# FFN weight tiles turned by a transposing DMA on 16-bit planes, in place of TensorE transposes

## The chip, the cores and the metric

The kernel runs on one core of a Trainium2 chip. The metric is the device time of one execution in microseconds. Five engines work beside each other: TensorE (PE in the profile; its weight loads are PEld), VectorE (DVE), ScalarE (ACT), GpSimd (POOL) and SyncE (SP), which here only issues DMAs. Each engine runs its own instruction list in order and waits on semaphores for the others.

## The reference

One transformer layer on x of 2048 tokens x 1024 features, in float32. First attention across the 32 heads of each token, then a gated FFN whose weights go through a 4-bit quantization and back:

```python
x = x + attn(layernorm(x), wq, bq, wk, bk, wv, bv)
dq(w): per block of 64 values: absmax, idx = searchsorted(bounds, w / absmax), NF4_CODE[idx] * absmax
g, u = y @ dq(w1).T, y @ dq(w2).T          # y = layernorm(x); w1, w2: 2752 x 1024
x = x + (silu(g) * u) @ dq(w3).T           # w3: 1024 x 2752
```

Quantizing and restoring the weights (w1, w2 and w3) is part of the work, and TensorE needs the restored weights transposed.

## The kernel before, in words

**Attention sweep.** The 16 token tiles of 128 rows are swept one after another: layer norm, transposes of the normed rows, q, k and v projections, scores, softmax, weighted sum, residual (`S`, `G`, `keep` and their callers; lines 610 to 865). L770 is the transpose of one tile's attention output on DVE, one for each token tile.

**FFN.** The hidden dimension of 2752 is cut into 21 chunks of 128 and one of 64, in six groups of up to four chunks. For each group and each half of the tokens, `Unit` (line 1406) multiplies chunk by chunk; a unit is seven products of four matmuls each (a Strassen-like scheme, `mm4` at L391), and its last operation on DVE is the multiply at L1451. `down7` (line 1509) multiplies the group's result with the third weight and sends the parts through ACT copies (L1532) and accumulating DMAs of POOL (L1534) into `x1d`. Unit operands come by SP's DMAs: `load_w12` (L458, L459) into two buffers, `load_op` (L446) for x.

**The weights, in the background.** A generator, `background()` (line 283), prepares 65 weight tiles, in an order of jobs ("1", c), ("2", c), ("3", c) and one joint ("12", 21). For each tile:

- `load_w` (L188 to L201) loads 128 x 1024 values into `wn` (three buffers), two jobs ahead.
- `absmax` (L264) takes each block's maximum (L271) and scales the tile by its reciprocal (L259 on ACT, L255 on DVE).
- Eight bands follow: ACT rounds to int8 (L299), DVE adds and clips (L303 for the first, L305 for the others) into `r` (two buffers).
- `scaled` multiplies `r` by the maxima, and `finish` (line 205) is put on a list of pending work.

`finish` transposes `r` on PE in eight 128x128 pieces (L219), four to a PSUM bank, and ACT copies each half into `wop` (L220; one buffer of eight 128x512 slots). After the second weight of a pair, DVE forms four sums (L226 to L229, L232 to L235), and SP stores the slots into a DRAM tile `wd` (L238). Units load from `wd` later.

**The order.** PE's list is the program's order, written by hand. On the other engines a scheduler decides the order when the program is built. The sweep and the units call `advance(n)`, which lets the background take steps at a fixed rate for the PE work just issued, and `flush`, which takes one step of `finish`; each step that issues transposes therefore has its fixed place in PE's list. `until(kind, c)` takes steps until a weight is there.

`hook["scale"]` names the engine that scales `r`: ACT in the attention sweep, then ACT and DVE in turn ("both"), and DVE inside `down7`.

The lines that the change touches:

```python
for half in range(2):
    pt = hook["psum"](half)
    for k in range(4):
        j = 4 * half + k
        nc.tensor.transpose(pt[:q, k, :], v[:, j * q : (j + 1) * q], ident)
    nc.scalar.copy(o[:q, first + half], pt[:q])
    yield
```

Of the kernel before, what the change touches and what calls it, by code (L numbers as in the profile page):

```python
# [20 lines left out]
P = 128  # L21
# [30 lines left out]
NNEG = 7  # L52
I8 = mybir.dt.int8
I32 = mybir.dt.int32
F32R = mybir.dt.float32r
LOW = 0xFFF

# [34 lines left out]
def preln_block_kernel(  # L92
# [22 lines left out]
    c = {"ident": ident, "eps": eps, "mhalf": mhalf}  # L115
    c["flag"] = const.tile([1, 1], I32, name="flag")
    io = (x, wqT, wkT, wvT, qb, kb, vb, w1, w2, w3, out)
# [13 lines left out]
def forward(ctx, tc, const, fast, x, wqT, wkT, wvT, qb, kb, vb, w1, w2, w3, out):  # L131

    nc = tc.nc
    xf = x.flatten_outer_dims()
    of = out.flatten_outer_dims()
    ident, eps, mhalf = const["ident"], const["eps"], const["mhalf"]
# [15 lines left out]
    hook = {"scale": "ACT"}  # L152
# [7 lines left out]
    def behind(kind):  # L160

        last = urgent["last"]
        return tc.issue_after(last) if last and kind in urgent["rule"] else nullcontext()
# [24 lines left out]
    def load_w(kind, c):  # L188
        h0, hn = c * P, min(P, F - c * P)
        t = dqp.tile([P, E], FP, tag="wn", name="wn", bufs=3)  # L190
        if kind == "3":
            nc.sync.dma_start(
                t[:, : KC * hn].rearrange("p (k h) -> p k h", h=hn),
                w3[:, h0 : h0 + hn].rearrange("(k p) h -> p k h", p=P),
            )
        elif kind == "12":
            nc.sync.dma_start(t[:hn, :], w1[h0 : h0 + hn, :])
            nc.sync.dma_start(t[hn : 2 * hn, :], w2[h0 : h0 + hn, :])
        else:
            nc.sync.dma_start(t, (w1 if kind == "1" else w2)[h0 : h0 + hn, :])  # L200
        return t  # L201

    wops = {}

    def finish(kind, c, v):

        hn = min(P, F - c * P)
        q = hn if kind == "3" else P
        paired = kind == "3" and c < PAIRED
        second = kind == "2" or paired and c % 2  # L210
        if not second:
            wops["t"] = dqp.tile([P, 8, 4, P], FP, tag="wop", name="wop", bufs=1)
        o = wops["t"]
        first = 2 if second else 0
        for half in range(2):
            pt = hook["psum"](half)
            for k in range(4):
                j = 4 * half + k
                nc.tensor.transpose(pt[:q, k, :], v[:, j * q : (j + 1) * q], ident)  # L219
            nc.scalar.copy(o[:q, first + half], pt[:q])  # L220
            yield
        if kind == "1" or paired and not second:
            return
        if paired:
            b11, b12, b21, b22, t1, t2, t3, t4 = (o[:, n] for n in range(8))
            nc.vector.tensor_tensor(t1, b12, b11, ALU.subtract)  # L226
            nc.vector.tensor_tensor(t2, b22, t1, ALU.subtract)
            nc.vector.tensor_tensor(t3, b22, b12, ALU.subtract)
            nc.vector.tensor_tensor(t4, b21, t2, ALU.subtract)  # L229
        if kind == "2":  # L230
            a11, a12, a21, a22, s1, s2, s3, s4 = (o[:, n] for n in range(8))
            nc.vector.tensor_tensor(s1, a21, a22, ALU.add)  # L232
            nc.vector.tensor_tensor(s2, s1, a11, ALU.subtract)
            nc.vector.tensor_tensor(s3, a11, a21, ALU.subtract)
            nc.vector.tensor_tensor(s4, a12, s2, ALU.subtract)  # L235
        n = 8 if second else 2
        d = tc.dram_tile([q, n, 4, P], FP, name=f"wd{kind}_{c}")
        nc.sync.dma_start(d, o[:q, :n])  # L238
        wd[kind, c] = d
        if paired:  # L240
            wd[kind, c - 1] = d

    pending, step = [], {}
# [6 lines left out]
    def scaled(dst, src, by, nb, engine):  # L250

        if engine == "DVE":
            d, s = (a.rearrange("p (b e) -> p b e", e=BLOCK) for a in (dst, src))
            f = by[:, :nb].unsqueeze(2).to_broadcast([P, nb, BLOCK])
            nc.vector.tensor_tensor(d, s, f, ALU.mult)  # L255
            return
        with behind("scale"):
            for n in range(nb):
                nc.scalar.mul(dst[:, ts(n, BLOCK)], src[:, ts(n, BLOCK)], by[:, n : n + 1])  # L259

    def width(kind, c):
        return KC * min(P, F - c * P) if kind == "3" else E

    def absmax(kind, c, wn):  # L264

        w = width(kind, c)
        nb = w // BLOCK
        v = wn[:, :w]
        am = fs.tile([P, 16], FP, tag="am", name="am")
        rc = fs.tile([P, 16], FP, tag="rc", name="rc")[:, :nb]  # L270
        nc.vector.tensor_reduce(  # L271
            am[:, :nb],
            v.rearrange("p (b e) -> p b e", e=BLOCK),
            AX.X,
            ALU.max,
            apply_absolute_value=True,
        )
        nc.vector.scalar_tensor_tensor(rc, am[:, :nb], 0.0, am[:, :nb], ALU.is_equal, ALU.add)
        nc.vector.reciprocal(rc, rc)  # L279
        scaled(v, v, rc, nb, "DVE" if hook["scale"] == "DVE" else "ACT")  # L280
        return am

    def background():
        ready = load_w(*jobs[0])
        ahead = load_w(*jobs[1])
        am = absmax(*jobs[0], ready)
        yield
        for n, (kind, c) in enumerate(jobs):
            wn, wa = ready, am
            ready = ahead  # L290
            if n + 2 < len(jobs):
                ahead = load_w(*jobs[n + 2])
            w = width(kind, c)
            v = wn[:, :w]
            r = dqp.tile([P, E], FP, tag="r", name="r", bufs=2)[:, :w]
            for i, (lo, hi, scale, bias) in enumerate(BANDS):
                t = dqp.tile([P, E], I8, tag="sg", name="sg", bufs=6)[:, :w]
                with behind("step"):
                    nc.scalar.activation(t, v, AF.Copy, bias=bias, scale=scale)  # L299
                top = float(NF4_CODE[hi + 1])  # L300
                low = -1.0 if lo is None else float(NF4_CODE[lo])
                if i == 0:
                    nc.vector.tensor_scalar(r, t, top, low, ALU.min, ALU.max)  # L303
                else:
                    nc.vector._custom_dve(TENSOR_ADD_SAT, out=r, in0=r, in1=t, s0=top, s1=low)  # L305
                step["n"] = i
                yield
                if i == 4 and n + 1 < len(jobs):
                    am = absmax(*jobs[n + 1], ready)
                    yield  # L310
            engine = ("ACT", "DVE")[n % 2] if hook["scale"] == "both" else hook["scale"]
            scaled(r, r, wa, w // BLOCK, engine)
            pending.append(finish(kind, c, r))
            yield

    def low_bits():

        acc = dqp.tile([P, E], FP, tag="r", name="acc", bufs=2).bitcast(I32)
        chunks = [(m, k) for m in (wqT, wkT, wvT) for k in range(KC)]
        got = []  # L320

        def load():
            if chunks:
                m, k = chunks.pop(0)
                t = dqp.tile([P, E], FP, tag="wn", name="wn", bufs=3)
                nc.sync.dma_start(t, m[ts(k, P), :])
                got.append(t.bitcast(I32))

# [19 lines left out]
    def chain():  # L348
        yield from background()
        if fast:  # L350
            yield from low_bits()
# [179 lines left out]
    if fast:  # L531
# [22 lines left out]
        def load_W(m):  # L554

            W[m] = [
                (wpool if tag in XTAGS else wv).tile([P, 2, E], F32R, tag=tag, name=f"w{m}{n}")
                for n, tag in enumerate(TAGS[m])
# [51 lines left out]
        def split(i):  # L610

            hi = work.tile([P, KC, P], F32R, tag="xh", name="xh", bufs=2)
            lo = work.tile([P, KC, P], F32R, tag="xl", name="xl", bufs=2)
            src = xn.pop(i)
# [293 lines left out]
    else:  # L908
# [190 lines left out]
        with tc.issue_after(opening["first"]):  # L1099
            for n in range(2):  # L1100
                k = slice(2 * n, 2 * n + 2)
# [4 lines left out]
        for n in range(2):  # L1106
            k = slice(2 * n, 2 * n + 2)
# [27 lines left out]
        def load_A(src, p):  # L1135
            t = pair.tile([P, 7, 4, P], FP, tag="A", name="A", bufs=2)
            nc.sync.dma_start(t, src[p])
            return t

        for p in range(NP):  # L1140
# [33 lines left out]
            if p == NP - 2:  # L1174
                first = load_A(opD, 0)
# [463 lines left out]
    for n, (g, tbp) in enumerate(passes):  # L1639
        half, sides = None, []  # L1640
        while now is not None and now.tbp == tbp and now.c in g:
# [6 lines left out]
            if g[-1] == NFULL and unit.c == NFULL - 1:  # L1648
                half = Half(tbp)
# [61 lines left out]
```

## Time and profile before

| | |
|---|---|
| median of 3 runs | 2228.09 us (2227.78 to 2230.97) |
| the profiled execution | 2224.73 us |
| its span, first to last instruction | 2222.9 us |
| granted TensorE clock, mean | 0.983 |
| PE busy | 2144.0 us (96%) |
| weight loads | 1148.3 us (52%) |
| DVE busy | 1395.8 us (63%) |
| ACT busy | 1302.8 us (59%) |
| POOL busy | 275.4 us (12%) |
| DMA, mean rate | 181 GB/s, 402.73 MB |

The busy time of an engine is the time in which at least one of its instructions ran. A group of the profile is a source line, an engine, an operation and the shapes; it has the count, the busy time, the mean duration of one in nanoseconds, and the idle time of that engine just before these instructions with what ended it ("<-PE ptw L219": the transposes of line 219). A view by stretches gives the busy time of each engine between two moments, for all instructions or for one line. The view of waits gives for each waiting line and each releasing line the total, the number of times and the longest.

### The profile page before, as it was taken

The page shows a single profiled execution, that of the slowest core. Times are in us where ns is not written, and L with a number is a line of the kernel's source. Part 1 is how long each engine was busy: PE and PEld are TensorE (multiplying, and loading weights), DVE is VectorE, ACT ScalarE, POOL GpSimd, SP SyncE. Part 2 cuts the span into 40 slices and gives each one's busy share as a digit, 9 for nine tenths or more (in the row PEclk, how much of TensorE's full clock was granted, in tenths as well). Part 3 has the DMA queues.
Part 4 walks back from the last instruction along what each step waited for, and adds up shares of the span by engine and source line. Part 5 has one row for each costly group of instructions (what it writes and reads, how often), then busy time and mean ns, then how long its engine had stood idle before and what let it go on. Part 6 is the DMA issues. An engine that isn't in the chain of part 4 may idle for free.

```text
span 2222.9 us, 35192 instructions
## 1 busy us (share of the span) xinstructions
PE 2144.0 (96%) x14193; PEld 1148.3 (52%) x14193; DVE 1395.8 (63%) x1599; ACT 1302.8 (59%) x2635; POOL 275.4 (12%) x335
## 2 busy tenths in 40 slices
PE   7899989898999999999999999999999999999998
PEld 6677777776544444444444444444444444444432
DVE  6788877978666567565665756756656656453022
ACT  7667665756656657657657676586575676411200
POOL 1000000000003104013021030030120310401300
PEclk8899999999999999999999999999999999999999
DMA  8132323324669539579377694494983866965972
GB/s 294 40 126 68 116 68 107 119 85 160 239 240 263 140 123 250 191 266 196 125 196 190 247 243 133 148 224 165 320 181 123 182 173 256 259 208 141 259 286 96
DMA packets 154684, 402.73 MB, mean 181 GB/s; under 512 B 13648, under 2 KB 67920, under 8 KB 137360
## 3 DMA queue, kind: packets, MB, share of 16 engines
q1 hardware_dynamic: 113808, 326.92, 40.9%
q0 software_dynamic: 40704, 73.47, 19.6%
q8 instruction: 113, 1.85, 0.3%
q14 instruction: 59, 0.48, 0.1%
HBM read 227.07 MB, written 173.28 MB: 180 GB/s over the span
## 4 chain that ended last, share of the span: by engine, by line
PE 44%; issue 21%; DMA 5%; POOL 2%; DVE 1%; ACT 1%; POOLq 0%; SPq 0%; DVEq 0%; ACTq 0%
PE z L391 17%; PE q L391 8%; PE z L1519 7%; DMA x1d<-acc 4%; PE rr L391 4%; PE y L1519 4%; POOL x1d L1534 2%; PE r L1519 2%; PE po L1602 1%; PE ptw L219 1%; PE po L1613 1%; DMA wn<-in_wqT_dram 0%; DVE r L305 0%; ACT acc L1532 0%; DMA w<-wd 0%
## 5 line engine op out<-in xcount | busy, mean ns | idle before, releaser
L299 ACT ACTIVATE sg<-wn 128x1024 int8<-128x1024 f32 (+1 forms) x520 | 541.8, 1050 | 100.0 <-DVE r L305 87.8
L305 DVE CUSTOM_DVE_ANT_0 r<-r,sg 128x1024 f32<-128x1024 f32 (+1 forms) x455 | 552.0, 1213 | 22.2 <-ACT sg L299 1.6
L1534 POOL DMA_DIRECT2D x1d<-acc x280 | 243.9, 900 | 1247.0 <-ACT acc L1532 1196.8
L391 PE MATMUL z<-xB,w 128*128 128x512 f32 x720 | 323.4, 599 | 8.8 <-DMA w<-wd 4.9
L391 PE MATMUL z<-xT,w 128*128 128x512 f32 x656 | 294.9, 592 | 0.0
L391 PE MATMUL q<-xT,w 128*128 128x512 f32 x656 | 291.3, 592 | 0.0
L1519 PE MATMUL z<-w,h 128*128 128x512 f32 x496 | 231.2, 594 | 3.2 <-ACT acc L1532 3.0
L259 ACT ACTIVATE wn<-wn,rc 128x64 f32<-128x64 f32 x752 | 192.6, 336 | 62.6 <-DVE rc L279 59.1
L391 PEld LDWEIGHTS z<-xB,w 128*128 128x128 f32 x720 | 135.9, 192 | 170.8 <-issue 157.7
L391 PEld LDWEIGHTS q<-xT,w 128*128 128x128 f32 x656 | 123.3, 190 | 149.5 <-issue 147.6
L391 PEld LDWEIGHTS z<-xT,w 128*128 128x128 f32 x656 | 123.0, 190 | 146.8 <-issue 146.1
L1434 DVE TENSOR_TENSOR g<-g,rr 128x512 f32<-128x512 f32 x41 | 27.9, 681 | 210.3 <-PE rr L391 210.2
L220 ACT COPY wop<-ptw 128x512 f32<-128x512 f32 (+1 forms) x130 | 76.1, 586 | 134.8 <-PE ptw L219 122.8
L1519 PEld LDWEIGHTS z<-w,h 128*128 128x128 f32 x496 | 92.4, 190 | 115.4 <-issue 101.2
L303 DVE TENSOR_SCALAR r<-sg 128x1024 f32<-128x1024 int8 (+1 forms) x65 | 44.8, 689 | 169.2 <-PE ptw L219 152.8
L1519 PE MATMUL y<-w,h 128*128 128x512 f32 x320 | 148.8, 592 | 0.0
L391 PE MATMUL rr<-xB,w 128*128 128x512 f32 x328 | 147.5, 592 | 0.0
L1532 ACT COPY acc<-z 128x512 f32<-128x512 f32 x160 | 92.9, 581 | 84.8 <-PE z L1519 48.2
L259 ACT ACTIVATE r<-r,am 128x64 f32<-128x64 f32 x440 | 112.8, 341 | 5.2 <-DVE r L305 4.8
L648 PE MATMUL pj<-wk,xh 128*128 128x512 f32 x224 | 94.1, 420 | 14.8 <-DVE qd L667 14.6
L271 DVE TENSOR_REDUCE am<-wn 128x16 f32<-128x1024 f32 (+1 forms) x65 | 78.3, 1204 | 39.8 <-ACT r L259 37.1
L391 PEld LDWEIGHTS rr<-xB,w 128*128 128x128 f32 x328 | 61.5, 190 | 73.7 <-issue 73.7
(144 smaller groups left out, 2749.2 us busy)
## 6 DMA issues: line engine op xcount, KB each, us to landing
x1d<-acc POOLq DMA_DIRECT2D x280, 256.0 KB, 7.0
wd<-wop SPq DMA_DIRECT2D x31, 2048.0 KB, 9.0
w<-wd SPq DMA_DIRECT2D x41, 1280.0 KB, 7.0
wn<-in_w_dram SPq DMA_DIRECT2D x63, 512.0 KB, 6.1
xT<-xdT SPq DMA_DIRECT2D x28, 1024.0 KB, 7.1
xB<-xdB SPq DMA_DIRECT2D x24, 1024.0 KB, 7.3
w<-wd SPq DMA_DIRECT2D x44, 512.0 KB, 4.1
w<-wd SPq DMA_DIRECT2D x10, 1536.0 KB, 7.3
```

The costliest lines, as they stand in the source:

```text
L220: nc.scalar.copy(o[:q, first + half], pt[:q])
L259: nc.scalar.mul(dst[:, ts(n, BLOCK)], src[:, ts(n, BLOCK)], by[:, n : n + 1])
L271: nc.vector.tensor_reduce(am[:, :nb], v.rearrange("p (b e) -> p b e", e=BLOCK), AX.X, ALU.max, apply_absolute_value=True,)
L299: nc.scalar.activation(t, v, AF.Copy, bias=bias, scale=scale)
L303: nc.vector.tensor_scalar(r, t, top, low, ALU.min, ALU.max)
L305: nc.vector._custom_dve(TENSOR_ADD_SAT, out=r, in0=r, in1=t, s0=top, s1=low)
L391: nc.tensor.matmul(dst, w[:, k, :], xop[:, k, :], start=start and k == 0, stop=stop and k == 3, skip_group_check=True,)
L648: nc.tensor.matmul(ps, part[:, k, :], W[m][k // 2][:, k % 2, ts(n, TB)], start=k == 0 and part is xs[i][0], stop=k == KC - 1 and part is x ...
L1434: nc.vector.tensor_tensor(self.g0, self.g0, r, ALU.add)
L1519: nc.tensor.matmul(dst, side[n][:, ts(q, P)], w3T[g[2 * m]][:, W3[n]], start=start and m == 0, stop=stop and m == 1, skip_group_check=True,)
L1532: nc.scalar.copy(t, src)
L1534: nc.gpsimd.dma_start(x1d[8 * tbp + 2 * q + j][n], t, accum_op=ALU.add)
```

## The change

For the 63 full tiles (not the joint tile of the two 64-row ends, nor the last 64 columns of the third weight), `finish` no longer uses PE. ACT reads `r` as 16-bit halves and writes the low halves of all values, then the high halves, into the tile's old `wn` buffer: two planes of 1024 halves. SP issues one transposing DMA from there into two slots of `wop` that are free at that time. A copy on POOL (while `hook["scale"]` is ACT) or on DVE (otherwise) puts the halves together again into the slots where PE's result used to go. The number of steps of `finish` is the same. `wn` now stays in use until the transposing DMA has read it.

```diff
-    def finish(kind, c, v):
+    def finish(kind, c, v, wn):
...
-        for half in range(2):
-            pt = hook["psum"](half)
-            for k in range(4):
-                j = 4 * half + k
-                nc.tensor.transpose(pt[:q, k, :], v[:, j * q : (j + 1) * q], ident)
-            nc.scalar.copy(o[:q, first + half], pt[:q])
+        if hn == P:
+            planes = wn.bitcast(U16).rearrange("p (two e) -> p two e", two=2)
+            turned = o[:, first + 4 : first + 6].rearrange("p n k d -> p (n k d)").bitcast(U16)
+            nc.scalar.copy(planes, v.bitcast(U16).rearrange("p (e two) -> p two e", two=2))
+            nc.sync.dma_start_transpose(
+                turned.rearrange("p (j h) -> p j h", h=P), wn.bitcast(U16)
+            )
             yield
+            joins = nc.gpsimd if hook["scale"] == "ACT" else nc.vector
+            joins.tensor_copy(
+                o[:, first : first + 2].rearrange("p n k d -> p (n k d)").bitcast(U16)
+                .rearrange("p (e two) -> p two e", two=2),
+                turned.rearrange("p (two e) -> p two e", two=2),
+            )
+            yield
+        else:
+            for half in range(2):
+                pt = hook["psum"](half)
+                for k in range(4):
+                    j = 4 * half + k
+                    nc.tensor.transpose(pt[:q, k, :], v[:, j * q : (j + 1) * q], ident)
+                nc.scalar.copy(o[:q, first + half], pt[:q])
+                yield
...
-            pending.append(finish(kind, c, r))
+            pending.append(finish(kind, c, r, wn))
```

More of the change, by code (lines that the diff above doesn't have):

```diff
@@ L54 @@
 I32 = mybir.dt.int32
+U16 = mybir.dt.uint16
 F32R = mybir.dt.float32r
```

## The prediction

> **What bounds the kernel now.** I read the busy time of each engine over four stretches first, then the same stretches for the TensorE transposes of line 219, then the groups of instructions, then who waited for whom. I cut the span at the sixth attention-output transpose (L770, 254.1 us), the first closing multiply of an FFN unit (L1451, 636.2) and the 23rd (1436.6): W1 and W2 are attention, W3 and W4 the FFN.
>
> ```profile
> 0.00:254.10 254.10, 225.47 (x3889) 180.80 (x3890) 202.41 (x224) 172.99 (x375) 18.03 (x36) 0.92 0.39 132
> 254.10:636.20 382.10, 354.29 (x6348) 263.14 (x6347) 303.17 (x329) 232.62 (x510) 13.45 (x19) 0.98 0.41 138
> 636.20:1436.60 800.40, 797.20 (x2039) 363.95 (x2038) 505.63 (x592) 524.95 (x1025) 121.88 (x140) 1.00 0.67 193
> 1436.60:2222.90 786.30, 767.01 (x1920) 340.37 (x1918) 384.57 (x460) 372.26 (x726) 122.04 (x140) 0.99 0.71 206
> ```
>
> After the length come PE, weight loads, DVE, ACT, POOL (busy us), granted clock, DMA share, GB/s. PE is busy 797 of 800 us in W3 and 767 of 786 in W4: there a microsecond taken off PE is a microsecond of the kernel. In W2 it is 354 of 382, with DVE at 303 (79%) beside it. DVE and ACT have 37% and 34% to spare in W3, 21% and 39% in W2.
>
> ```profile
> 0.00:254.10 254.10, 5.37 (x32) 4.13 (x32) 0.92 0.39 132
> 254.10:636.20 382.10, 10.19 (x68) 8.48 (x68) 0.98 0.41 138
> 636.20:1436.60 800.40, 37.32 (x248) 30.83 (x248) 1.00 0.67 193
> 1436.60:2222.90 786.30, 25.80 (x172) 21.37 (x172) 0.99 0.71 206
> ```
>
> These are line 219 alone: 520 transposes, 78.7 us of PE, 0.151 each.
>
> ```profile
> L219 PE MATMUL ptw<-ident,r 128*128 128x128 f32 x512 | 77.5, 274 | 3.8 <-DVE vd L680 2.0 <-ACT wop L220 1.8
> L220 ACT COPY wop<-ptw 128x512 f32<-128x512 f32 x128 | 75.0, 586 | 128.1 <-PE ptw L219 116.1 <-DMA wd<-wop 12.0
> L303 DVE TENSOR_SCALAR r<-sg 128x1024 f32<-128x1024 int8 x64 | 44.2, 691 | 160.1 <-PE ptw L219 152.8 <-ACT wn L259 7.3
> L299 ACT ACTIVATE sg<-wn 128x1024 int8<-128x1024 f32 x512 | 536.9, 1056 | 98.2 <-DVE r L305 85.9 <-DVE r L303 4.9 <-ACT acc L1532 1.0
> L568 DVE CAST wq<-stage 128x1024 fp32r<-128x1024 f32 x4 | 2.8, 690 | 5.1 <-DMA stage<-in_wqT_dram 5.1
> ```
>
> The reader should stop at L303: DVE sat idle 152.8 us because the first band of the next weight tile waits until PE has transposed an older one out of the two buffers of `r`. PE's order is fixed by hand, so **the transposes are also the pace-maker of the dequantization**, and they go.
>
> **The change, part by part.** The instruction lists of the two programs say what it issues. PE loses 504 of 520 transposes (63 full tiles; the 64-row ones stay): 504 x 0.151 = 76.3 us. PE alone would then need 254.1 - 5.4 = 249, 382.1 - 10.2 = 372, 800.4 - 37.3 = 763 and 786.3 - 23.4 = 763 (the 16 that stay, 2.4 us, are in W4): 2147 in all.
>
> ACT loses 126 copies (0.586 us each, 74 us) and gains 63 splits of 2048 halves. L299 gives 1.056 us for 1024 elements and 0.633 for 512, so a straight line gives 1.9; bounds 1.06 (if halves went at double rate) and 2.1; I take 1.9, as no ACT row shows a faster rate. ACT +46 us.
>
> The joins read 2048 halves and write every second one: 52 on DVE, 11 on POOL. DVE's nearest row is L568 (one SBUF input): 0.690 for 1024, where two-input adds take 0.69 for 512 and 1.22 for 1024, so twice their rate. Bounds: 0.69 (rate doubled again) and 2.29 (single rate); I take 1.22, L568's rate. DVE +63 us. On POOL the fills and selects of 128x128 took 204 and 322 ns against about 100 for one column: 0.8 to 1.7 ns an element, so 1.8 to 3.7 us; I take 1.8, a copy being nearer to a fill.
>
> The transposing DMA moves 512 KB. Plain loads of that size land in 3.8 (xt) to 6.1 us (wn). Above: if it went in 256-byte pieces, it would be 2048 packets; queue q1 spent 0.409 x 16 x 2222.9 / 113808 = 0.128 us of one engine on a packet, so 16.4 us on 16 engines. I take 6, the row of equal size. SP issues 63 more (0.33 us each, 21 us), and in its list a load of `wn` mostly stands right behind a transpose and waits for it to land, since the tile is now reused for the halves. Behind that load stand stores of x1, loads of w and of x operands. The cover: w has two buffers, and a freed one is needed four products later (16 x 0.59 = 9.5 us), with 4.1 to land, so 5.4 us. A 6 us hold stays about within it: I cost it at nothing. Beyond 5.4 us it costs PE directly.
>
> The Trainium skill speaks against the trade: "VectorE: DVE Perf Modes", section "The three transpose paths", gives 390 ns for a 128x128 16-bit transpose on TensorE and 1309 ns by DMA. A tile is 16 such blocks, so an estimate by that page is 20.9 us a tile if they follow one another, and the sum would be the third rival's; no row of this trace has a transposing DMA.
>
> **What moves** decides the sum. No weight transposes order the background any more, and the scheduler packs it earlier: before the first L1451 the DVE list starts 22 tiles (L303) instead of 14, before the 23rd 64 of 65 instead of 45. I added row durations (overlaps taken out) along the changed lists between the same marks. DVE: 224, 386, 693 and 147 us; ACT: about 180, 311, 702 and 143. Engines run in list order, so a PE-critical add now stands behind filler whether or not that filler is needed.
>
> W1: DVE's 224 fits under 249. W2: DVE's 386 exceeds PE's 372, so **DVE becomes the bound in W2**, and its waits come on top. W3: 693 and 702 against 763, over 90% each.
>
> ```profile
> DVE xU L527 <- DMA xdT<-xU: 22.4, 9, 4.3
> DVE prT L745 <- ACT pr L743: 6.0, 3, 2.7
> DVE h L1446 <- ACT si L1445: 36.9, 11, 6.3
> DVE h L1440 <- ACT u L1438: 35.9, 11, 5.9
> DVE am L271 <- ACT r L259: 21.2, 7, 5.9
> ACT sg L299 <- DVE r L305: 46.8, 89, 4.9
> ACT wn L259 <- DVE rc L279: 20.8, 18, 3.6
> ACT g L1435 <- DVE g L1434: 20.7, 7, 3.7
> ```
>
> These are waits of W2 (first two lines, asked from 250 us on) and W3 that do not come from PE; I assume that a busier engine does not shed them. W2: 386 + 22 + 6 + 11 joins x 1.8 (DVE's sums at L232 to L235 stand behind POOL's join) = 434. W3: DVE 693 + 94 = 787, ACT 702 + 88 = 790; I take 790. W4 has little filler left: PE's 763. Sum: 249 + 434 + 790 + 763 = 2236 of span against 2222.9. The profiled execution took 2224.73, 1.8 outside its span; the median, 2228.09, is 3.4 above it. So 2236 + 1.8 + 3.4 = **2241 us, slower by 0.6%**: W1 and W4 gain 28, W3 10, W2 loses 52.
>
> "SBUF — State Buffer", section "Who interferes with whom", says that a GpSimd instruction that reads SBUF and a VectorE one with two SBUF inputs exclude each other for their whole length. An estimate from it puts up to 11 x 1.8 = 20 us more on DVE in W2, and the sum at 2261; POOL's present rows touch at most one column of SBUF beside DVE, so nothing here shows it.
>
> **The rivals.** *PE sets the pace throughout (faster).* DVE and ACT waits are mostly filled by the denser list, and only W2 is held by DVE's bare 386: 249 + 386 + 763 + 763 = 2161, 2166 with the two offsets; with half of my added waits about 2204. For it: W3 leaves PE 60 us of slack over either engine, and the 152.8 us at L303 vanish. Against: W2 has none. Its range is 2152 to 2220.
>
> *Even.* W2's loss equals the rest's gain: 434 less 8 does it. 2224 to 2232.
>
> *The transposing DMA is the bound (slower).* If it takes 16.4 us, SP is held 63 x 16.4 = 1033 us, some 78% of the 21 us that a tile has in W2 and W3 (56 tiles in 1182 us). A w load then waits about 8 us in most units, some 5 beyond what the cover leaves after landing: 41 x 5 = 205 on top of 2152, about 2350. It decides from 5.4 us. For it: DMA is already 67% busy in W3. Against: same bytes as a 6 us load.
>
> That the change does not do what it says is excluded by the lists: the 504 transposes are gone.
>
> **How the numbers follow.** Forecast case (2233 to 2320) 0.44, PE paces 0.36, even 0.10, DMA bound 0.10. So faster by over 0.2% 0.36, within 0.2% 0.10, slower 0.54; 0.2% is about what a measurement of this kernel can tell from no change. Range: the top adds the join's upper bound, 51 x 1.07 = 55 us, and the 27.4 us that ACT waits on x1d stores in W3: 2323, so 2320. The bottom takes in the bare sum of the faster rival, 2166, so 2165. Left out: the best of the faster rival (0.08) and the DMA case. Cases of both signs hold most of the chance; the forecast's own range is 2233 to 2320.
>
> **What would show it.** In the changed profile: PE under 95% in W2 with its waits on DVE lines (L667, L680, L745); DVE over 92% busy until the first L1451, which comes near 680 us instead of 636; PE near 97% in W3, and 23 us gained after the 23rd L1451. The split near 1.9 us and the join near 1.22 on DVE. Wrong if the first L1451 comes before 640 (the faster rival), if PE waits on w loads behind SP, or if the transposing DMA lands much later than 6 us.

## The result, and the profile after

The changed kernel takes **2389.97 us** (median of 4 runs, 2379.77 to 2394.68) against 2227.94 us before on the same chip (4 runs, 2226.94 to 2230.97): a ratio of 1.070, 95% interval 1.068 to 1.073. It is 7% slower. The prediction was 2241 us, 0.6% slower, and its range ended at 2320: the sign held, the size did not. The profiled execution has a span of 2377.9 us.

The same four stretches, cut at the same instructions (the sixth L787, which was L770; the first and the 23rd L1468, which was L1451; lines behind `finish` are shifted by 17). Columns as in the prediction: length, PE, weight loads, DVE, ACT, POOL, granted clock, DMA share, GB/s.

```profile
0.00:271.00 271.00, 227.62 (x3863) 181.61 (x3864) 224.82 (x248) 206.64 (x450) 39.59 (x43) 0.91 0.48 147
271.00:691.70 420.70, 360.84 (x6281) 262.06 (x6280) 382.81 (x420) 301.51 (x601) 34.44 (x23) 0.94 0.54 162
691.70:1609.20 917.50, 795.85 (x1793) 342.64 (x1792) 674.63 (x785) 677.43 (x1270) 128.72 (x142) 0.94 0.83 215
1609.20:2377.90 768.70, 746.26 (x1757) 323.92 (x1755) 149.52 (x203) 144.41 (x252) 119.24 (x138) 0.99 0.65 170
```

| stretch | before | predicted | after | after less predicted |
|---|---|---|---|---|
| W1 | 254.1 | 249 | 271.0 | +22 |
| W2 | 382.1 | 434 | 420.7 | -13 |
| W3 | 800.4 | 790 | 917.5 | **+127.5** |
| W4 | 786.3 | 763 | 768.7 | +6 |

W3 carries the miss. No engine is the bound there: DVE and ACT are at 74%, PE at 87%. What stands out is the DMA share, 0.83 instead of 0.67. Within W3, the units take as long as before (22 to 30 us from one closing multiply to the next, 23 to 28 before); the five intervals that hold a `down7` take 92, 97, 95, 83 and 115 us instead of 75, 74, 77, 74 and 75. That is 108 of W3's 117 us. So the place is `down7`, and the view to ask is the table of engines over these five intervals, first of the kernel before, then of the changed one.

```profile
687.00:761.00 74.00, 73.04 (x188) 33.06 (x187) 46.43 (x50) 57.08 (x112) 23.64 (x27) 1.00 0.87 206
837.00:911.00 74.00, 73.01 (x189) 33.31 (x188) 51.05 (x54) 57.34 (x103) 23.66 (x28) 1.00 0.92 225
985.00:1062.00 77.00, 76.15 (x196) 34.74 (x195) 51.03 (x56) 60.74 (x117) 24.21 (x28) 1.00 0.89 217
1136.00:1209.00 73.00, 73.00 (x187) 33.29 (x186) 42.74 (x48) 54.33 (x109) 24.18 (x28) 1.00 0.93 228
1285.00:1360.00 75.00, 74.60 (x189) 33.81 (x188) 42.72 (x49) 58.56 (x126) 24.23 (x28) 1.00 0.89 214
```

```profile
742.00:835.00 93.00, 75.10 (x170) 32.51 (x169) 53.00 (x61) 62.45 (x126) 24.91 (x27) 0.91 0.97 204
909.00:1006.00 97.00, 75.05 (x169) 31.77 (x168) 67.69 (x75) 72.91 (x125) 24.54 (x28) 0.91 0.96 215
1083.00:1179.00 96.00, 73.39 (x166) 31.65 (x165) 47.06 (x56) 62.48 (x143) 23.49 (x26) 0.89 0.95 194
1255.00:1338.00 83.00, 73.66 (x161) 31.98 (x161) 55.21 (x62) 66.91 (x125) 23.67 (x27) 0.94 1.01 236
1414.00:1529.00 115.00, 75.40 (x159) 32.02 (x159) 59.92 (x69) 59.81 (x111) 25.86 (x28) 0.82 0.82 177
```

Look at the last column but one. In `down7` the 16 DMA engines were 87 to 93% busy **before the change**; the 0.67 that the prediction quoted is a mean over units at about half of that and `down7` at nine tenths. Length times share, summed over the five, is 336 us of all DMA engines before and 453 after: 117 us more DMA time, in intervals that are 111 us longer. The table of DMA queues (packets, MB, share of 16 engines' span) gives what one transposing DMA needs; q1 is SP's queue, before and after:

```profile
q1 hardware_dynamic: 113808, 326.92, 40.9%
```

```profile
q1 hardware_dynamic: 244848, 359.96, 48.3%
```

The share times the span was 909 us (0.409 x 2222.9) before and is 1149 (0.483 x 2377.9) after, so 3.8 us of all 16 engines for each of 63. The trace shows 20 begun inside the five intervals, and two more less than 5 us ahead of one of them, so by this estimate some 80 of the 117 us are theirs.

How that reaches PE is seen at 737 us in the timelines of SP, DVE, ACT and PE (start, us, engine, line, operation; in brackets the idle time ahead and its releaser).

```profile
737.49 29.48 SPq L220 DMA_TRANSPOSE wop<-wn  x2
767.07 7.25 SPq L201 DMA_DIRECT2D wn<-in_w_dram  x2
```

```profile
762.49 1.32 DVE L225 COPY wop<-wop 128x2048 uint16<-128x2048 uint16 x1 [15.15 <-DMA wop<-wn]
...
773.99 1.31 DVE L225 COPY wop<-wop 128x2048 uint16<-128x2048 uint16 x1 [9.46 <-DMA wop<-wn]
...
778.36 0.24 DVE L296 RECIPROCAL rc<-rc 128x16 f32<-128x16 f32 x1
```

```profile
778.64 1.06 ACT L276 ACTIVATE wn<-wn,rc 128x64 f32<-128x64 f32 x4 [16.30 <-DVE rc L296]
...
781.28 0.56 ACT L1549 COPY acc<-z 128x512 f32<-128x512 f32 x1
```

```profile
781.90 3.78 PE L1536 MATMUL z<-w,h 128*128 128x512 f32 x4 [15.80 <-ACT acc L1549]
```

SP stays 29 us inside two transposing DMAs. DVE stands 15 and 9 us at the two joins. The next tile's absmax and reciprocal come behind them in DVE's list, ACT waits 16 us for the reciprocal, and behind that scaling stands the PSUM copy of `down7` that PE needs to go on: PE stands 15.8 us. The waits of W3 (total, times, longest) show the same links; before the change, PE waited for that copy only 4.0 us in the whole span. First the line of the kernel before, then those of the changed one:

```profile
PE z L1519 <- ACT acc L1532: 4.0, 7, 1.1
```

```profile
DVE wop L225 <- DMA wop<-wn: 156.8, 29, 28.3
PE z L1536 <- ACT acc L1549: 87.0, 12, 21.0
ACT wn L276 <- DVE rc L296: 58.1, 9, 23.0
```

The costs of the new operations themselves:

```profile
L219 ACT COPY wn<-r 128x2048 uint16<-128x2048 uint16 x63 | 119.3, 1894 | 45.2 <-DVE r L272 34.0 <-DVE rc L295 11.1
L225 DVE COPY wop<-wop 128x2048 uint16<-128x2048 uint16 x52 | 69.0, 1327 | 170.6 <-DMA wop<-wn 170.3
L225 POOL COPY wop<-wop 128x2048 uint16<-128x2048 uint16 x11 | 30.7, 2792 | 177.1 <-DMA wop<-wn 159.4 <-DVE kd L684 17.7
```

And the view of the transposing DMA's line; its three durations are SP's stay inside the issue, at the least, in the middle and at the most:

```profile
L220 SPq DMA_TRANSPOSE wop<-wn x63: 1317/3279/18327, 60.1 to 2082.7; - x63
...
DMA to landing us min/median/max: 4.2/5.6/33.4
```

The split (predicted 1.9 us), the join (1.22 and 1.8) and the landing in the middle (6) are near what was predicted. The issue is not: 0.33 us was taken, 272 us in all stand there instead of 21, and the tails of 18 and 33 us belong to DMAs that run in `down7`.

### The profile page after: what moved, and what is told of

The parts are those of the page before. It is cut to its first block, busy times and chain, and to the rows that moved or that the text cites. A ratio compares the mean times of both kernels' runs of the same rounds, so it can differ in the third digit from the quotient of the medians.

```text
span 2377.9 us, 34295 instructions
## 1 busy us (share of the span) xinstructions
PE 2130.6 (90%) x13689; PEld 1110.2 (47%) x13689; DVE 1431.8 (60%) x1651; ACT 1330.0 (56%) x2572; POOL 322.0 (14%) x346
## 3 DMA queue, kind: packets, MB, share of 16 engines
q0 software_dynamic: 40704, 73.47, 19.2%
## 4 chain that ended last, share of the span: by engine, by line
PE 35%; DMA 8%; issue 6%; DVE 5%; ACT 4%; SPq 0%; DVEq 0%; POOL 0%; ACTq 0%; POOLq 0%
PE z L408 13%; PE z L1536 7%; PE q L408 6%; DMA wop<-wn 4%; PE y L1536 3%; PE rr L408 3%; DVE r L322 2%; PE r L1536 2%; DMA wn<-in_w_dram 2%; PE po L1619 1%; ACT sg L316 1%; ACT wn L276 1%; DMA x1d<-acc 1%; PE po L1630 1%; DMA wn<-in_wvT_dram 1%
## 5 line engine op out<-in xcount | busy, mean ns | idle before, releaser
L322 DVE CUSTOM_DVE_ANT_0 r<-r,sg 128x1024 f32<-128x1024 f32 (+1 forms) x455 | 551.7, 1217 | 38.4 <-ACT sg L316 27.4
L316 ACT ACTIVATE sg<-wn 128x1024 int8<-128x1024 f32 (+1 forms) x520 | 519.4, 1046 | 75.9 <-DVE r L322 29.4
L1551 POOL DMA_DIRECT2D x1d<-acc x280 | 248.0, 904 | 1356.0 <-ACT acc L1549 1225.2
L408 PE MATMUL z<-xT,w 128*128 128x512 f32 x656 | 303.1, 606 | 33.3 <-ACT u L1448 23.9
L1536 PE MATMUL z<-w,h 128*128 128x512 f32 x496 | 238.8, 612 | 67.7 <-ACT acc L1549 67.7
L1451 DVE TENSOR_TENSOR g<-g,rr 128x512 f32<-128x512 f32 x41 | 28.0, 683 | 310.7 <-PE rr L408 310.7
L225 DVE COPY wop<-wop 128x2048 uint16<-128x2048 uint16 x52 | 69.0, 1327 | 170.6 <-DMA wop<-wn 170.3
L219 ACT COPY wn<-r 128x2048 uint16<-128x2048 uint16 x63 | 119.3, 1894 | 45.2 <-DVE r L272 34.0
L1448 ACT COPY u<-z 128x512 f32<-128x512 f32 x41 | 23.7, 577 | 175.2 <-PE z L408 175.2
L276 ACT ACTIVATE r<-r,am 128x64 f32<-128x64 f32 x440 | 112.5, 337 | 13.2 <-DVE r L322 13.1
L665 PE MATMUL pj<-wk,xh 128*128 128x512 f32 x224 | 100.1, 447 | 20.0 <-DVE qd L684 19.3
```

The source lines that it names most:

```text
L219: nc.scalar.copy(planes, v.bitcast(U16).rearrange("p (e two) -> p two e", two=2))
L225: joins.tensor_copy(o[:, first : first + 2].rearrange("p n k d -> p (n k d)").bitcast(U16) .rearrange("p (e two) -> p two e", two=2), turn ...
L408: nc.tensor.matmul(dst, w[:, k, :], xop[:, k, :], start=start and k == 0, stop=stop and k == 3, skip_group_check=True,)
L665: nc.tensor.matmul(ps, part[:, k, :], W[m][k // 2][:, k % 2, ts(n, TB)], start=k == 0 and part is xs[i][0], stop=k == KC - 1 and part is x ...
L1451: nc.vector.tensor_tensor(self.g0, self.g0, r, ALU.add)
L1536: nc.tensor.matmul(dst, side[n][:, ts(q, P)], w3T[g[2 * m]][:, W3[n]], start=start and m == 0, stop=stop and m == 1, skip_group_check=True,)
```

## The experiments

**A: the DVE wait.** The first theory was that the join is the cause: DVE stands in order for a late DMA, and the stall passes to ACT and PE. Its rivals were **B**, the background is packed too densely once nothing on PE paces it, and **C**, SP's list holds the transposes and they hold SP's loads. The kernel before, run beside the next four, took 2232.6 us (median).

`e1_plain`: the same bytes by a plain DMA.

```diff
-            nc.sync.dma_start_transpose(
-                turned.rearrange("p (j h) -> p j h", h=P), wn.bitcast(U16)
+            nc.sync.dma_start(
+                turned, wn.bitcast(U16)
             )
```

> Every transposing DMA is replaced by a plain DMA of the same 512 KB from the same tile to the same place, on the same queue; the weights then come out unturned, so the output is not the reference's. The scheduler may place DVE's and ACT's filler otherwise, PE's order stays. Theory A (the join stands in DVE's list for a DMA that in down7 is held 15 to 18 us in its issue on SP and lands after 20 to 33 us): issue and landing fall to about 0.1 and 6 us, DVE's 170 us at the join fall under 40, the stretch between the first and the 23rd L1468 goes from 917 to 790 to 820 us, and the kernel to 2240 to 2280. Theory B (without transposes on PE the background is packed too densely for DVE and ACT, whatever moves the halves): still 2350 or more, with the waits at other lines. Theory C (the DMA is late because it stands in SP's list behind loads and stores that wait): the hold inside the issue goes but the 10 to 38 us between split and issue stay, about 2310 to 2350.

Measured: 2283.6 us, ratio 1.022 (1.020 to 1.024). The issue takes 0.47 us, the landing 3.4 in the middle and 17.8 at the most. W3 is 827 us, the `down7` intervals 80 to 83. The time and W3 lie just above what A allowed (2280 and 820), and DVE still waits 53 us at the joins, not under 40. So 4.8 of the 7.0% belong to the DMA being a transposing one. The other 2.2% do not: the first closing multiply stays at 686 us, which is the side of theory B.

`e2_pooljoin`: `joins = nc.gpsimd` for all tiles.

> All 63 joins on GpSimd (2.8 us each there), so that DVE holds no instruction that waits for the transposing DMA except the sums of a pair. Theory A: DVE's 170 us at the join go, a part comes back at the sums (19 pairs), the stretch between the first and the 23rd L1468 goes from 917 to 820 to 870 us, the kernel to 2290 to 2340. Theory B: 2370 or more, since DVE sheds only 69 us of work. Theory C: SP is held as before, so the wd stores and wn loads come as late, 2360 to 2390, with PE waiting for w.

Measured: 2415.4 us, ratio 1.082 (1.081 to 1.084), above what A and C gave; B had said 2370 or more. In the waits of its W3 DVE no longer stands at the join, but GpSimd does, and its list holds the accumulating DMAs of `down7`:

```profile
POOL wop L225 <- DMA wop<-wn: 438.9, 36, 26.7
POOL x1d L1551 <- ACT acc L1549: 176.2, 63, 30.2
...
ACT acc L1549 <- DMA x1d<-acc: 69.4, 23, 13.1
```

The wait moved into another in-order list, and ACT now waits 69 us (16.8 with the change as it was) for its buffers to be stored. A second cost comes with it: DVE sheds 69 us of joins and yet is busy for 1431.7 us, as long as before that (1431.8), since its instructions with two inputs in SBUF take longer beside the joins (the mean of L322 is 1304 ns instead of 1225). So the run does not tell the three theories apart.

`e3_attn` and `e4_ffn`: the new path only until the units begin, and only from there on (`hook["ffn"]` is set where the units' PSUM pools are made). The edit of the first is shown; the second has no `not`.

```diff
-        if hn == P:
+        if hn == P and not hook.get("ffn"):
```

> Transposing DMA only for the tiles finished before the FFN units begin; from there on TensorE turns them as in the kernel before. Theory A and C: the attention stretches stay at 271 and 421 us (the loss of 56 us there is DVE's content), the FFN has no late DMA and goes back to 800 plus 786 us or less, as some 8 tiles more are done by then: 2250 to 2290. Theory B, if it is the pace set by PE that matters: the pace is back in the FFN only, same 2250 to 2290; but if the attention's loss came from DVE standing at joins there, the first L1468 would move back under 660.

> TensorE turns the weights until the FFN units begin, the transposing DMA from there on. All theories: the first closing multiply comes back to about 636 us. Theory A and C: the stretch between the first and the 23rd L1468 is as long as with the whole change, 900 to 950 us, and as the background is less advanced then, some of its loss goes on behind the 23rd, 2330 to 2400. Theory B: with the earlier filler gone from attention, the FFN has more of it: also 2330 to 2400, but with DVE and ACT over 90% busy in the stretch instead of 74%.

Measured: `e3_attn` 2239.5 us, ratio 1.002 (1.000 to 1.004), below the 2250 to 2290 that all theories gave: nearly nothing is lost, the first closing multiply is at 644 us. It turns 12 tiles by DMA in attention (the changed kernel 20), landing in 4.3 to 8.4 us, and starts 14 tiles before that mark, as before the change. So a join and a DMA for each of 12 tiles cost 8 us at most; most of the attention's 55 us go with the eight tiles more that the unpaced list packs there (B). `e4_ffn`: 2353.1 us, ratio 1.054 (1.052 to 1.056); its five `down7` intervals in W3 take 97, 90, 102, 82 and 113 us. DVE and ACT are 76% busy there, not over 90%, as B wanted.

**B, and the sum of the causes.** The kernel before took 2236.9 us beside these.

`e5_pace`: one TensorE transpose a tile, whose result nobody uses, ahead of the split.

```diff
         if hn == P:
+            nc.tensor.transpose(hook["psum"](0)[:q, 0, :], v[:, :q], ident)
             planes = ...
```

> The whole change plus one 128x128 transpose on TensorE for each full tile, ahead of the split, whose result nobody uses: it reads r and so gives the background its old pace. DVE's list then starts 15 tiles before the first closing multiply and 46 before the 23rd (14 and 45 in the kernel before, 22 and 64 with the change); PE gets 63 x 0.15 = 9.5 us of the 76 back. Theory B (the loss is the dense packing): first closing multiply back at 636 to 650 us, the stretch to the 23rd at 770 to 800, the kernel at 2150 to 2200. Theory A and C (in the FFN the loss is the transposing DMA, held on SP and landing late in down7): the first mark comes back as under B, but the down7 stretches of 74 us stay at 85 to 100, now also behind the 23rd, where filler is left: 2270 to 2370.

Measured: 2340.9 us, ratio 1.047 (1.043 to 1.050), as A and C expected. The first mark comes back to 656.6, short of the 650 expected, and all ten `down7` now take 76 to 100 us (72 to 77 before the change).

`e6_actq`: `nc.scalar.dma_start_transpose`.

> The transposing DMAs are issued by ScalarE instead of SP; all else stays (the density as well, 22 and 62 tiles). Theory C (SP's list is what holds the transposes, and the transposes what hold SP's loads): the 10 to 38 us between split and issue go, SP's loads are free, ACT carries the 272 us of issue in its idle time: 2280 to 2330. Theory A in its plain form (the transposing DMA itself is slow against the traffic of down7, wherever it is issued): landings of 20 to 30 us stay, and as ACT now stands in the issue for up to 18 us with the copies that release PE behind it, 2390 to 2450. Theory B: unchanged, 2370 to 2400.

Measured: 2419.4 us, ratio 1.084 (1.080 to 1.088). The landings reach 29.1 us and the issue 15.4 us on ACT's queue too. So the late landing does not come from SP's list, and C falls as the cause of it; ACT's stay in the issue has its own price, so what SP's stay adds in the changed kernel is not known from this run.

`e7_mix`: as `e5_pace`, with `hn == P and hook["scale"] != "DVE"` as the condition.

> As e5_pace, but inside down7 TensorE turns the tiles as in the kernel before (about 25 of 63), and the transposing DMA does so elsewhere. Theory A and C: with no transposing DMA begun in down7 its stretches go back to 75 us, PE sheds about 38 x 7 x 0.15 = 40 us, of which the attention's part is hidden: 2190 to 2225, faster than both kernels. Theory B: the same as e5_pace within 20 us, as the density is the same.

Measured: 2228.4 us, ratio 0.996 (0.994 to 0.998): slightly faster than before, by less than expected, since the attention still loses 24 us (first mark 660). 44 tiles go by DMA, and 15 of them still begin in an interval of `down7` (25 in `e5_pace`), but none lands later than 12.2 us. With 19 tiles fewer by DMA than `e5_pace` it is 112 us faster, and the ten `down7` intervals together are 114 us shorter (749 instead of 863): some 6 us for each tile that TensorE turns again.

`e8_late`: two more `yield` ahead of the join.

> The join comes two steps of the background later, so that DVE has more work between the split and the join. Theory A (DVE stands at the join, ACT behind it, PE behind ACT): DVE's 170 us at the join go under 100 and the kernel to 2300 to 2350. Theory B and C: 2370 to 2400; under C the time that DVE no longer stands at the join comes back at the sums and at late wn loads, since SP is held as before.

Measured: 2366.0 us, ratio 1.058 (1.055 to 1.061). DVE stands at the join for 128 us instead of 170, and waits of 59 us for the loads of `wn` appear. Below what B and C expected and above A: where the join stands is worth about 1%, and not the loss.

**The last link.** The kernel before took 2237.1 us beside these.

`e9_both_only`: as `e5_pace`, with the condition `hn == P and hook["scale"] == "both" and hook.get("ffn")`.

> The transposing DMA only for tiles that finish inside the FFN but outside down7 (about 32), with the one pacing transpose each; TensorE turns all others as in the kernel before. All theories but B: the attention is that of the kernel before (first closing multiply at 636 to 645 us), the stretch to the 23rd stays at 790 to 802, the rest at 767 to 775: 2195 to 2220, faster than both kernels. Theory B (density) gives the same, as the density is that of before; if the transposing DMA costs wherever it stands in the FFN, 2235 or more.

Measured: 2212.3 us, ratio **0.990** (0.988 to 0.993), faster than both kernels. Its stretches, 0 to the first closing multiply, to the 23rd, and to the end:

```profile
0.00:637.50 637.50, 579.22 (x10235) 443.00 (x10236) 506.53 (x550) 409.66 (x887) 32.81 (x55) 0.96 0.40 134
637.50:1438.00 800.50, 785.15 (x1902) 350.82 (x1901) 533.92 (x621) 540.09 (x1007) 123.00 (x142) 1.00 0.80 211
1438.00:2204.90 766.90, 752.66 (x1834) 330.52 (x1832) 390.50 (x463) 373.24 (x709) 120.16 (x139) 0.99 0.79 215
```

The first two are as before; the last is 19 us shorter, and PE has 14 us less to do there. With 32 tiles turned by DMA this is the fastest of all kernels that were run with the change in it. Its five `down7` intervals in W3:

```profile
687.00:761.00 74.00, 71.09 (x184) 32.47 (x183) 44.62 (x51) 53.73 (x102) 22.39 (x26) 1.00 0.94 202
837.00:918.00 81.00, 73.26 (x179) 32.93 (x178) 49.02 (x55) 53.07 (x106) 22.71 (x27) 0.96 0.97 201
992.00:1067.00 75.00, 75.00 (x188) 33.92 (x187) 51.62 (x58) 57.35 (x112) 23.68 (x27) 1.00 0.97 210
1143.00:1216.00 73.00, 73.00 (x184) 33.05 (x184) 35.88 (x43) 49.30 (x101) 22.82 (x27) 1.00 1.00 192
1292.00:1363.00 71.00, 71.00 (x179) 32.23 (x178) 36.54 (x44) 50.62 (x103) 23.15 (x27) 1.00 0.95 191
```

Nine transposing DMAs begin in them, instead of 20 in the changed kernel. The DMA engines are 94 to 100% busy, and yet only one interval is longer than before. So a high DMA share alone is not the loss; in the changed kernel it comes with instructions that wait in order for a late transfer.

`e10_no_x1d`: the accumulating DMA of `down7` (L1551) replaced by `pass`.

> The whole change, without the 280 accumulating DMAs of down7 (the sum of the parts is left out, so the output is not the reference's). Theory A1 (the transposing DMA lands late because its packets share the DMA engines with the accumulating traffic of down7): the issues in down7 fall from 15 to 18 us to under 5 and the landings from 20 to 33 us to under 9, the down7 stretches from 92 to 115 us to 72 to 80, the kernel to 2250 to 2290. Theory A2 (the collision is with SP's own loads of operands and weights, on the same queue): issues over 10 us and landings over 20 us stay, the stretches stay over 85, and the kernel falls only by what ACT waits for the accumulating DMAs, under 30 us, 2350 to 2390.

Measured: 2244.3 us, ratio 1.004 (1.002 to 1.007). Its W3 and its first `down7`:

```profile
692.50:1481.00 788.50, 777.38 (x1796) 338.49 (x1795) 674.07 (x784) 676.03 (x1270) 0.00 (x0) 1.00 0.64 203
743.00:813.00 70.00, 70.00 (x164) 30.97 (x163) 51.87 (x60) 61.24 (x125) 0.00 (x0) 1.00 0.53 155
```

On the side of A1, and further: the time is below its 2250, though the issue still reaches 11.1 us (it had said under 5) and one landing 13.2 (under 9). In the middle a landing takes 4.5 us, DVE stands 33 us at the joins instead of 170, PE is busy throughout that `down7`, and W3 takes 788.5 us, near the 790 of the prediction.

`e11_pace_plain`: `e5_pace` and `e1_plain` together.

> As e5_pace (one pacing transpose for each tile), with plain DMAs in place of the transposing ones (the weights come out unturned, so the output is not the reference's). With the changed kernel, e1_plain and e5_pace this makes a table of two by two: dense or paced, transposing or plain. Theory: both causes add up. Dense minus paced is 49 us with the transposing DMA (2390 against 2341), transposing minus plain 106 us when dense, so 2341 - 106 = 2235, between 2215 and 2255. If pacing alone cures the DMA's lateness or the plain DMA alone cures the density, it is outside of that, 2280 or more.

Measured: 2230.3 us, ratio 0.997 (0.996 to 0.999). The table of two by two, as ratios to before:

| | transposing DMA | plain DMA | difference |
|---|---|---|---|
| dense | 1.070 | 1.022 | 0.048 |
| paced | 1.047 | 0.997 | 0.050 |
| difference | 0.023 | 0.025 | |

Within their intervals the two causes add up: about 4.9% (109 us) for the transposing DMA, about 2.4% (54 us) for the dense packing.

`e12_traffic`: TensorE's transposes back, the DMA beside them, without a join.

```diff
+        if hn == P:
+            planes = ...
+            nc.scalar.copy(planes, ...)
+            for at in () if second else (4, 6):
+                turned = o[:, at : at + 2]...
+                nc.sync.dma_start_transpose(turned..., wn.bitcast(U16))
         for half in range(2):
...
```

> TensorE turns all tiles as in the kernel before, and beside that ScalarE splits every full tile and SP issues 64 transposing DMAs, two at the first tile of a pair, into slots that nobody reads before the sums of the pair overwrite them: the traffic without a join that waits for it. Theory A (the loss is DVE standing at the join, then ACT, then PE): down7 stays at 75 to 82 us, the kernel at 2235 to 2275 (119 us of splits in ACT's idle time). Rival (the packets themselves slow the other transfers, or SP's held list delays loads of w and x): down7 at 85 or more with PE waiting for w or x operands or for the accumulating DMAs, the kernel at 2290 to 2360.

Measured: 2430.3 us, ratio 1.087 (1.084 to 1.091). The rival's side, and above its 2360: A falls as it was put, since no instruction waits at a join here and the ten `down7` take 72 to 106 us. What DVE stands at now is the absmax of the next tile, 309 us for the loads of `wn`. SP, which issues these loads, stays inside the transposing DMAs for 328 us in all and waits another 57 us until they have read the `wn` that a load is to fill.

The accumulating DMAs (`e13`, `e14`), the rest of `e12`'s loss (`e15`) and the size of one DMA (`e16`) were open; beside the last four the kernel before took 2236.2 us.

`e13_before_no_x1d`: the kernel before with the same `pass`.

> The kernel before, without the 280 accumulating DMAs of down7 (the sum of the parts is left out, so the output is not the reference's): the control to e10_no_x1d. Theory A1 (the transposing DMA and the accumulating DMAs collide, neither is slow alone): the kernel before hardly gains, as PE is 97 to 100% busy in the FFN: 2200 to 2228, so that the changed kernel without that traffic stands 16 to 45 us above it, the part of the dense packing. Rival (the accumulating DMAs cost any kernel this much): it falls by 60 us or more, below 2170.

Measured: 2218.7 us, ratio 0.993 (0.990 to 0.995), as A1 expected: the kernel before gains 17 us without that traffic, the changed one 146, and the two then stand 26 us apart. Its five `down7` intervals show a DMA share of 0.30 to 0.36, so the accumulating DMAs hold some 57% of the DMA engines there.

`e14_x1d_write`: `accum_op=ALU.add` left out of L1551.

> The whole change, the 280 DMAs of down7 writing in place of adding (the output is not the reference's); the lists of all engines are those of the changed kernel, and as many bytes leave SBUF. If the adding is what collides: landings of the transposing DMA in down7 under 10 us, down7 stretches of 70 to 80 us, the kernel at 2245 to 2280. If the packets as such or GpSimd's queue collide: landings over 18 us and stretches over 85 us stay, 2340 to 2390.

Measured: 2294.9 us, ratio 1.025 (1.022 to 1.029), between the two expectations. The same bytes hold the DMA engines for 8.7% of the span instead of 19.2%, and the share in the five intervals is 0.75 to 0.84; they take 85, 78, 79, 77 and 82 us, and the landings reach 19 us. So what counts is how much DMA time the other stream leaves, and the adding is most of it, not all.

`e15_traffic_plain`: `e12_traffic` with plain DMAs.

> As e12_traffic, with plain DMAs in place of the 64 transposing ones: ScalarE's 119 us of splits, the held wn tiles and SP's waits stay. If e12's 190 us come from the transposing DMA itself: 2230 to 2275, down7 at 75 to 80 us. If they come from the splits on ACT or from the tile that is held longer: 2340 or more.

Measured: 2321.3 us, ratio 1.039 (1.036 to 1.042), between the expectations. 109 of `e12`'s 194 us are the transposing DMA, the same as in the table; the remaining 85 come with the splits on ACT, the held `wn` (DVE's absmax waits 201 us for its loads) and the plain DMA itself. These were not told apart.

`e16_four`: each transposing DMA cut in four.

```diff
+            for b in range(4):
-            nc.sync.dma_start_transpose(turned..., wn.bitcast(U16))
+                nc.sync.dma_start_transpose(turned...[:, ts(b, 4)], wn.bitcast(U16)[:, ts(b, 512)])
```

> The whole change, each transposing DMA cut in four of 128 KB. If the cost is by packets (as many as before): the four issues and the last landing take about as long as the one did, 2370 to 2400. If a fixed part of each DMA matters (its issue took 1.3 us at least): 63 x 3 x 1.3 = 246 us more in SP's list, 2410 to 2480. If short pieces let other transfers pass: 2300 to 2350.

Measured: 2450.4 us, ratio 1.097 (1.093 to 1.101). An issue takes 1.19 us at least and 1.27 in the middle, though it moves a quarter: each DMA has a fixed part, and W3 grows by 38 us. Short pieces do not help.

## Why the prediction was wrong

**Where it held.** W2: PE fell to 86%, DVE was 91% busy (88% up to the first closing multiply, where over 92% was forecast), and that multiply came at 691.7 us (near 680 was forecast, 640 would have refuted it): the denser packing does cost the attention, and `e5_pace`, with the old density, takes 35 of the 55 us back. The split, the join on DVE and the landing in the middle were sized within 9%; the join on POOL took 2.8 us instead of 1.8 (inside its bounds). W4 came within 6 us. W3 takes 788.5 us, near the 790 of the sum, once `down7`'s accumulating DMAs are away (`e10_no_x1d`). That is in part luck: the sum had DVE and ACT with their waits as the bound there, but PE is busy for 777.4 of these 788.5 us, DVE for 674.1. And that kernel's 2244 us meet the forecast of 2241 with 692.5 us up to the first closing multiply (683 forecast) and 758 behind the 23rd (763).

**The step that failed** is "A 6 us hold stays about within it: I cost it at nothing", with its inputs, 0.33 us for the issue and 6 us for the landing everywhere. That sum had one duration for the whole span, and the prediction's own sign of being wrong, a landing much later than 6 us, came in `down7`. In `down7` the DMA engines had 7 to 13% left, and a transposing DMA needs 3.8 us of all of them. Four of those in an interval are 15 us, where 5 to 10 of 74 were free. The step also asked only what stands behind SP; DVE's join, absmax and reciprocal, and ACT's PSUM copies behind them, carried the delay to PE (the 87 us above).

The price: the five intervals take 483 us, 406 with a plain DMA in its place (`e1_plain`), 377 with the plain DMA and the old density (`e11_pace_plain`) and 375 before. So 77 of the 108 us there belong to the transposing DMA and 29 to the dense packing. Over the whole kernel the transposing DMA costs 109 us. By this estimate 5 to 10 us of DMA time were missing in an interval; the transposing DMA cost 15 in each, and how that divides between the DMA engines and the waits on DVE, on ACT and in SP's list was not measured.

**The rival that was nearest in time failed in its place.** "The transposing DMA is the bound", about 2350 and given a chance of 0.10, named the right operation, and its 16.4 us for a landing with 256-byte packets lies inside what `down7` shows (4 to 33, 8.7 in the middle for the 20 begun there). But it put the cost on PE waiting for w loads behind SP in most units. The units kept their length, the waits of PE in W3 have none for w, and moving the issues off SP (`e6_actq`) made it worse. The argument against it, "same bytes as a 6 us load", is the error in one phrase: the plain DMA of the same bytes took 1.6 us of all DMA engines ((0.441 x 2284.4 - 909) / 63), the transposing one 3.8.

**W1** was predicted at 249, PE's work alone, and took 271, with neither PE (84%) nor DVE (83%) busy throughout. With the old density it is 260 us (`e5_pace`), with plain DMAs 261 (`e1_plain`). So each takes back half of the 22 us; which waits these are stays open.

**The two pages of the Trainium skill.** "VectorE: DVE Perf Modes", section "The three transpose paths", gives 1309 ns for a 128x128 block by DMA, and the estimate of 20.9 us a tile was far from the landings in attention, 4.3 to 8.8 us; only the latest in `down7` reach it. That the DMA path is the dear one held in `down7`, though not by that price. "SBUF — State Buffer", section "Who interferes with whom", held in kind: beside a GpSimd join, DVE's L322 (two inputs in SBUF) took up to 3.68 us instead of 1.21 in `e2_pooljoin`, while the absmax (one input) stayed at 1.22. In the changed kernel nine overlaps with L322 and L686 cost DVE some 6 us, all overlaps together some 10, not the 20 of the estimate.

## What to carry to other kernels

Ask the DMA share stage by stage before adding a transfer, as one does with the engines: 0.67 over W3 hid 0.9 in `down7`. Count a transfer by the time that it holds the DMA engines, not by its bytes, and then ask what waits in order behind it. And when work leaves the engine that paces the rest, price the pace apart from the work: here it cost 54 us, and one small instruction a tile gave it back. With that, and with TensorE turning the tiles of the attention and of `down7` as before, the change was worth 1%.

## What the runs showed of the hardware

- A transposing DMA of 512 KB from SBUF to SBUF makes 2080 packets (131,040 more on the SP queue for 63), nearly all under 512 bytes; the plain one makes 144 (9072 more). 14 times as many packets show in DMA time as 3.8 against 1.6 us. On ACT's queue (`e6_actq`), where nothing else runs, the same 3.8 us come out directly (0.098 x 2416.0 / 63); without the accumulating DMAs it is 3.3 (`e10_no_x1d` against `e13_before_no_x1d`).
- The queue that issues it is inside the instruction for 1.3 to 23.4 us (the most in `e4_ffn`), 3.3 us in the middle; a plain DMA took 0.47. The stay grows with the load on the DMA engines: without the accumulating DMAs its sum fell from 272 to 186 us.
- The 280 accumulating DMAs of 256 KB hold the DMA engines for 1.6 us each (0.192 x 2377.9 / 280); the same as plain writes, 0.7.
- Where PE stood in `down7`, its granted clock fell, to 0.82 in the interval of 115 us, and the four matmuls after the stall shown above took 3.78 us, where others take 1.88.
